# Group means by ScalarE, denominators written before they are read back, and the last blocks added ahead, in four fused layers

## The chip, the cores and the metric

One core of a Trainium2 chip. The kernel is one program that runs four layers one after the other. The time is the device time of an execution in microseconds (us), the median of three runs. The profile is that of one execution.

A core has five engines that run their own instruction streams in order and wait for each other through semaphores: TensorE (PE, matrix products; PEld is its loading of weights), VectorE (DVE), ScalarE (ACT), GpSimd (POOL) and SyncE (SP), which here mostly issues transfers (DMA). Products are written to PSUM, eight banks of 128 x 512 float32; everything else lives in SBUF, 128 partitions wide.

## The reference, cut to what matters

The input is two images of 512 channels and 32 x 32 pixels, float32. Layer 0 is an attention with sampled keys and a small network for its position bias, followed by an MLP; the change leaves its first part alone. Then come

```python
# layer 1: group norm, 8 heads of 64 channels, softmax over 1024 pixels, projection, residual
g = (g - mean) * rsqrt(var + EPS)              # over groups of 16 channels x 1024 pixels
w = softmax(q^T k / sqrt(64)); hh = w v
x = x + proj_w hh + proj_b
# layer 2: group norm, one head of 512 channels
x = x + w_proj softmax(q^T k / sqrt(512)) v + b_proj
# layer 3: no norm, q and k of 64 channels, softmax over the query axis
x = gamma * o + x
```

## The kernel before, in words

Channels lie on partitions, four blocks of 128 (`CC` = 4), and the 1024 pixels (`HW`) along the free axis, in two halves of 512 (`HALF`) or four quarters of 256 (`QUARTER`). All matrix products are float32; each is two records on PE in the profile. Most large products are done by a Strassen-like scheme with seven products instead of eight (`group`, L1463): four PSUM banks x, y, v, z; a product into each, copies and sums of partial results by ACT and DVE (`p1`, `u2`, `p5`, `u3`), then three more products into x, y and v, and an `evict` that adds up the four blocks of the result.

The order of work is written by hand. `in_order` keeps every engine in program order, so an instruction that waits holds all that stand behind it on its engine. What DVE has to do beside the evictions (sums for the seven products, norms, divisions) is put into lists called tracks as (cost, function) pairs with waits between them (a bare number, in us of a virtual clock). `do_chores` is called between products; it advances that clock and issues from each track what is ready, up to a budget of DVE time. So moving or adding one chore shifts what comes after it on its track, and what the other tracks get of the budget.

The places that the change touches:

- `group_norm` (L1212) is a generator. It takes statistics per channel, then forms group means by a product with a constant matrix (`over_group`, L1222): the product goes to a PSUM bank `pg`, the generator yields, and at the next call DVE copies it to `gm` or `var` (L1227). Until then the bank is taken. After the variance, an inverse root is found by four Newton turns of three small DVE operations (L1246), and scale and shift follow. In attention and layer 2 a track made by `statistics` (L1539) advances the generator, with a wait of 6 or 3 us after each late step; in the MLP of layer 0 it is advanced every second chunk.
- `attend` (L1636) is layer 1's attention: 16 iterations, each with eight score products (two 64-row heads side by side), eight exponentials by ACT into tiles of `arena`, and the value products of the iteration before. `divide` (L1687) gets the softmax denominators: products with ones sum over partitions (`den`), ACT copies the rows, four small transfers spread them over partitions (`few`), DVE inverts (`invert`, L1708), the result is written to DRAM (`d`) and read back to 64 partitions each (`r`). Then DVE multiplies `o` by `r`. Of the two halves each is written and read back in turn, all on SP's queue.
- `Weights.total` (L1927) and `divisor` (L1947) do the same for layers 2 and 3. In layer 2 (`shares` False) the exponentials are first added up on DVE to one tile `acc`, and `den` is two products with 512 columns, in two groups of 32 PE columns. It runs four times.
- `weighed` (L1984) is the product of values and weights. Its very last call, second image, second half, second group, uses `evict_last` (L1989): for four 128 x 256 blocks it adds the bias `gb3` and the residual x and where there is one the partial sum, in turn, and stores 128 x 512 blocks to the output with `done` (L2132).

At the end all engines read a flag (is the fast softmax safe?), branch past a general version and meet at a barrier.

Of the kernel before, what the change touches and what calls it, by code (L numbers as in the profile page):

```python
# [12 lines left out]
F32 = mybir.dt.float32  # L13
AF = mybir.ActivationFunctionType
ALU = mybir.AluOpType
# [4 lines left out]
P = 128  # L20
B, C, H, W = 2, 512, 32, 32
HW = H * W
CC = C // P
HALF = 512
# [55 lines left out]
def kernel(ctx: ExitStack, tc: tile.TileContext, a: dict, out: bass.AP):  # L80
    nc = tc.nc
# [14 lines left out]
    def cs(name, i=None):  # L96
        lo, hi = _CONST_AT[name]
        return cst[:, lo:hi] if i is None else cst[:, lo + i : lo + i + 1]
# [1097 lines left out]
    def layers(f, fold_d, t2_b, o2_b, left1, right1):  # L1196
# [3 lines left out]
        small = f.enter_context(tc.tile_pool(name="small", bufs=2))  # L1200
# [11 lines left out]
        def group_norm(x, gname, bname, h, small_psum):  # L1212

            st = small.tile([P, CC, 2, 6], F32, name="st")
            mv = small.tile([P, CC, 2], F32, name="mv")
            for cc in range(CC):
                for half in range(2):
                    nc.vector.bn_stats(st[:, cc, half, :], x[:, cc, half * HALF : (half + 1) * HALF])
                nc.vector.bn_aggr(mv[:, cc, :], st[:, cc].rearrange("p h s -> p (h s)"))
                yield  # L1220

            def over_group(v, name):  # L1222
                pg = small_psum("pg")[:, :CC]
                nc.tensor.matmul(pg, cs("gmean"), v, start=True, stop=True)
                yield
                g = small.tile([P, CC], F32, name=name)
                nc.vector.tensor_copy(g, pg)  # L1227
                return g

            mean = small.tile([P, CC], F32, name="mean")  # L1230
            nc.vector.tensor_copy(mean, mv[:, :, 0])
            yield
            gm = yield from over_group(mean, "gm")
            nc.vector.tensor_sub(mean, mean, gm)
            nc.vector.tensor_mul(mean, mean, mean)
            nc.vector.tensor_add(mean, mean, mv[:, :, 1])
            yield
            var = yield from over_group(mean, "var")
            nc.vector.tensor_scalar(var, var, EPS, None, ALU.add)

            rs = small.tile([P, CC], F32, name="rs")
            square = small.tile([P, CC], F32, name="square")
            nc.vector.tensor_scalar(
                rs.bitcast(mybir.dt.int32), var.bitcast(mybir.dt.int32), -0.5, float(0x5F3759DF), ALU.mult, ALU.add
            )
            for _ in range(4):  # L1246
                nc.vector.tensor_mul(square, rs, rs)
                nc.vector.scalar_tensor_tensor(square, square, -0.5, var, ALU.mult, ALU.mult)
                nc.vector.scalar_tensor_tensor(rs, square, 1.5, rs, ALU.add, ALU.mult)
            sc = small.tile([P, CC], F32, name="sc")  # L1250
            sh = small.tile([P, CC], F32, name="sh")
            nc.vector.tensor_mul(sc, rs, col(gname, 0, CC))
            nc.vector.tensor_mul(sh, gm, sc)
            nc.vector.tensor_sub(sh, col(bname, 0, CC), sh)
            yield
            normed = chan.tile([P, CC, HW], F32, name="hc")
            h.append(normed)
            for cc in range(CC):
                nc.scalar.activation(
                    normed[:, cc, :], x[:, cc, :], AF.Identity, scale=sc[:, cc : cc + 1], bias=sh[:, cc : cc + 1]  # L1260
                )
                yield
# [136 lines left out]
        QUARTER = HALF // 2  # L1399
# [60 lines left out]
        def seven_right(b11, b12, b21, b22, t1, t2, t4, t3=None):  # L1460
            return b11, b21, b22, t4, t1, t2, b12 if t3 is None else t3

        def group(name, nk, n, stationary, moving, evict, slack, plain=False):  # L1463

            third = nk * n / 256

            x, y, v, z = [bank(name)[:, :n] for _ in range(4)]

            def add(out, l, r, start=True):
                for k in range(nk):  # L1470
                    nc.tensor.matmul(  # L1471
                        out,
                        stationary(l, k),
                        moving(r, k),
                        start=start and k == 0,
                        stop=k == nk - 1,
                        skip_group_check=not start,
                    )

            if plain:  # L1480
                for out, (l, r) in ((x, (0, 0)), (y, (6, 0)), (v, (0, 6)), (z, (6, 6))):
                    add(out, l, r)
                    add(out, 1 if l == 0 else 3, 1 if r == 0 else 2, False)
                evict((x, None), (v, None), (y, None), (z, None))
                return
            later, put_off[:] = list(put_off), []
            add(x, 0, 0)
            p1 = temp("p1", n)
            nc.scalar.copy(p1, x)
            if nk > 2:  # L1490
                add(z, 3, 3)
            add(y, 5, 5)
            u2 = temp("u2", n)
            nc.vector.tensor_tensor(u2, y, p1, ALU.add)
            add(v, 4, 4)
            p5 = temp("p5", n)
            nc.scalar.copy(p5, v)
            at_once(later)
            do_chores(third, slack)
            if nk == 2:  # L1500
                add(z, 3, 3)
            add(x, 1, 1, False)
            do_chores(third, slack)
            add(y, 6, 6, False)
            u3 = temp("u3", n)
            nc.vector.tensor_tensor(u3, y, p1, ALU.add)
            add(v, 2, 2, False)
            evict((x, None), (v, u2), (z, u3), (p5, u3))
            do_chores(third, slack)
# [28 lines left out]

        def statistics(steps, wait):  # L1539
            t = track()  # L1540
            for i in range(CC + 5):
                t.append((1.5 if i < CC else 0.5, lambda: advance(steps)))
                if i >= CC:
                    t.append(wait)
            return t
# [141 lines left out]
        def divide(o, acc):  # L1687
# [20 lines left out]
            def invert():  # L1708
                nc.vector.reciprocal(few, few)
                note(few)  # L1710
                d, r = sums_d.tile([2, HW], F32, name="d"), unit("r")
                held.append(r)
                for part in range(2):
                    i = slice(part * 64, part * 64 + 64)
                    nc.sync.dma_start(
                        out=d[part].rearrange("(h q n) -> q h n", h=2, q=64),
                        in_=few[i].rearrange("q (h n) -> q h n", h=2),
                    )
                    nc.sync.dma_start(out=r[i], in_=d[part].partition_broadcast(64))

            def scale():
# [173 lines left out]
        class Weights:  # L1895
# [31 lines left out]
            def total(self):  # L1927
                den, row = bank("den"), temp("row", HALF)
                some = [p.rearrange(self.order, k=2, q=2) for p in (self.p if self.shares else self.acc)]
                n = self.n = min(4, 2 * len(some))  # L1930
                self.few = small.tile([P, 4, HALF // P], F32, name="few2")
                for i in range(2 * len(some)):
                    j = i % n
                    nc.tensor.matmul(
                        den[32 * j : 32 * j + 32],
                        ones[:, :32],
                        some[i // 2][:, i % 2],
                        start=i < n,
                        stop=i + n >= 2 * len(some),
                    )  # L1940
                nc.scalar.copy(row[: 32 * n], den[: 32 * n])
                for i in range(n):
                    nc.sync.dma_start(
                        out=self.few[:, i], in_=row[32 * i : 32 * i + 1].rearrange("o (q n) -> o q n", q=P)
                    )
# [38 lines left out]
        def weighed(name, x, qb, seven_sv, w, bias, done=None, last=False):  # L1984

            n = slice(qb * HALF, (qb + 1) * HALF)
            for g in range(2):

                def evict_last(c11, c12, c21, c22):  # L1989
                    for (base, more), i, q in ((c11, 0, 0), (c21, 1, 0), (c22, 1, 1), (c12, 0, 1)):  # L1990
                        m, at = g + 2 * i, qb * HALF + q * QUARTER
                        dst = x[:, m, at : at + QUARTER]
                        if more is not None:
                            nc.vector.tensor_add(dst, dst, more)
                        nc.vector.scalar_tensor_tensor(dst, base, bias[:, m : m + 1], dst, ALU.add, ALU.add)
                        if q:
                            done(m, n)

                def evict(c11, c12, c21, c22):
                    c = unit("c").rearrange("p (m q n) -> p m q n", m=2, q=2)  # L2000
# [14 lines left out]

                group(
                    name, 4, QUARTER, lambda i, s: seven_sv(i, s)[:, g * P : (g + 1) * P], w.seven,
                    evict_last if last and g else evict, 2.6,
                )
                yield  # L2020

# [286 lines left out]
```

## Time and profile before

| | |
|---|---|
| median of three runs | 3342.02 us (3341.78 to 3342.47) |
| profiled execution | 3342.55 us, its span 3340.7 us |
| PE busy | 3316.0 us, 99% |
| DVE, ACT, POOL busy | 79%, 54%, 20% |
| granted PE clock | 0.999 |
| layer 0 with its MLP | to about 2410 us of the span |
| layer 1 | about 2410 to 2825 and its projection to 2889 |
| layers 2 and 3 | interleaved from 2825 to the end |

Lines of the profile name the source line, the engine and the operation, with the tiles it writes and reads. In the chain of waits, one follows from the last instruction back to what released it; start and length are in us. The wait list gives for each engine what it waited for: total us, times, longest. In the table of stretches a row gives the stretch, its length, and for each engine its busy us and number of instructions, then clock and DMA share. A PE "busy" time has modelled ends, so lengths between starts say more than busy sums.

### The profile page before, as it was taken

The page shows a single profiled execution, that of the slowest core. Times are in us where ns is not written, and L with a number is a line of the kernel's source. Part 1 is how long each engine was busy: PE and PEld are TensorE (multiplying, and loading weights), DVE is VectorE, ACT ScalarE, POOL GpSimd, SP SyncE. Part 2 cuts the span into 40 slices and gives each one's busy share as a digit, 9 for nine tenths or more (in the row PEclk, how much of TensorE's full clock was granted, in tenths as well). Part 3 has the DMA queues.
Part 4 walks back from the last instruction along what each step waited for, and adds up shares of the span by engine and source line. Part 5 has one row for each costly group of instructions (what it writes and reads, how often), then busy time and mean ns, then how long its engine had stood idle before and what let it go on. Part 6 is the DMA issues. An engine that isn't in the chain of part 4 may idle for free.

```text
span 3340.7 us, 60894 instructions
## 1 busy us (share of the span) xinstructions
PE 3316.0 (99%) x24789; PEld 1600.6 (48%) x24789; DVE 2642.5 (79%) x3033; ACT 1812.4 (54%) x2763; POOL 675.3 (20%) x806
## 2 busy tenths in 40 slices
PE   9999999999999999999999999999999999999999
PEld 4333333333333333333333339999953443687777
DVE  7999999999998899999999966455446465665556
ACT  4866877877876677877867642112136245122221
POOL 1333333333333233333333210000000000000000
PEclk9999999999999999999999999999999999999999
DMA  5887787787777587787787741000100000000111
GB/s 178 165 167 150 158 167 159 156 168 154 161 161 157 109 168 152 163 163 158 162 165 155 154 119 58 14 11 11 52 0 14 26 33 16 7 7 4 29 33 36
DMA packets 142993, 343.92 MB, mean 103 GB/s; under 512 B 36976, under 2 KB 51952, under 8 KB 141936
## 3 DMA queue, kind: packets, MB, share of 16 engines
q0 software_dynamic: 68400, 231.26, 37.1%
q1 hardware_dynamic: 71056, 102.12, 10.2%
q10 hardware_dynamic: 3248, 6.56, 0.5%
q8 instruction: 197, 3.23, 0.4%
q14 instruction: 92, 0.75, 0.1%
HBM read 71.46 MB, written 10.83 MB: 25 GB/s over the span
## 4 chain that ended last, share of the span: by engine, by line
PE 96%; DVE 1%; issue 1%; ACT 1%; DMA 0%; ACTq 0%; POOL 0%; DVEq 0%; POOLq 0%
PE z L630 52%; PE pma L135 6%; PE pw L1471 6%; PE pmb L135 5%; PE pmv L1471 4%; PE score L1650 3%; PE pv L1662 3%; PE pm L1471 3%; PE score L1471 3%; PE pmt L1471 1%; PE ppr L1471 1%; PE sim L659 1%; PE pf L135 1%; PE pp L719 1%; PE pma L1374 1%
## 5 line engine op out<-in xcount | busy, mean ns | idle before, releaser
L630 PE MATMUL z<-wa,cpb_w 128*32 128x512 f32 x10880 | 1192.2, 593 | 3.4 <-ACT h L639 3.4
L639 ACT ACTIVATE h<-z,b2h 128x1024 f32<-128x1024 f32 x768 | 852.1, 1115 | 329.2 <-PE z L630 300.4
L613 DVE CUSTOM_DVE_ANT_1 wa<-tab,pairs 128x2048 f32<-128x2048 f32 x340 | 779.9, 2295 | 2.9 <-PE z L630 2.5
L630 PEld LDWEIGHTS z<-wa,cpb_w 128*32 128x32 f32 x10880 | 346.2, 110 | 809.7 <-issue 713.6
L630 PE MATMUL z<-h,cpb_w 128*32 128x512 f32 x5504 | 609.4, 593 | 0.7 <-ACT h L639 0.7
L613 DVE CUSTOM_DVE_ANT_1 h<-tab,pairs 128x2048 f32<-128x2048 f32 x172 | 394.7, 2295 | 1.3 <-PE z L630 1.0
L630 PEld LDWEIGHTS z<-h,cpb_w 128*32 128x32 f32 x5504 | 175.6, 110 | 407.9 <-issue 364.3
L644 DVE SCALAR_TENSOR_TENSOR h<-h,turn,h 128x1024 f32<-128x1024 f32 x256 | 329.8, 1288 | 5.5 <-ACT h L639 5.5
L639 ACT ACTIVATE bridge<-z,b2h 128x1024 f32<-128x1024 f32 x162 | 181.1, 1118 | 118.6 <-PE z L630 118.6
L963 POOL DMA_DIRECT2D bridge<-bridge x150 | 127.6, 850 | 530.6 <-DMA bridge<-h 498.1
L644 DVE SCALAR_TENSOR_TENSOR bridge<-bridge,turn,h 128x1024 f32<-128x1024 f32 x162 | 208.3, 1286 | 5.2 <-ACT bridge L639 5.2
L970 POOL DMA_DIRECT2D bridge<-h x161 | 151.7, 942 | 289.3 <-DVE h L644 175.1
L1314 ACT COPY p<-pma 128x128 f32<-128x128 f32 x80 | 21.4, 267 | 334.4 <-PE pma L135 313.3
L1306 DVE TENSOR_TENSOR upper<-pma,p 128x256 f32<-128x256 f32 x80 | 33.8, 422 | 178.5 <-ACT p L1314 178.4
L1651 ACT ACTIVATE p<-score 128x512 f32<-128x512 f32 x256 | 130.3, 628 | 81.0 <-PE score L1650 79.9
L963 POOL DMA_DIRECT2D h2j<-h2j x90 | 76.2, 847 | 313.0 <-DMA h2j<-h 304.2
L639 ACT ACTIVATE h2j<-z,b2h 128x1024 f32<-128x1024 f32 x94 | 105.1, 1118 | 41.8 <-PE z L630 41.2
L1683 DVE TENSOR_TENSOR acc<-acc,p 128x1024 f32<-128x1024 f32 x96 | 111.2, 1219 | 19.8 <-ACT p L1651 19.5
L1650 PE MATMUL score<-q,k 64*128 64x512 f32 x512 | 120.7, 604 | 1.1 <-DVE gm L1227 1.1
L644 DVE SCALAR_TENSOR_TENSOR h2j<-h2j,turn,h 128x1024 f32<-128x1024 f32 x94 | 121.3, 1290 | 0.0
L1662 PE MATMUL pv<-p,vT 128*64 128x512 f32 x512 | 116.5, 598 | 0.0
L973 POOL DMA_DIRECT2D bridge<-bridge x90 | 108.4, 1204 | 3.2 <-DMA bridge<-bridge 2.5
(463 smaller groups left out, 4369.5 us busy)
## 6 DMA issues: line engine op xcount, KB each, us to landing
bridge<-h POOLq DMA_DIRECT2D x161, 512.0 KB, 5.2
h2j<-h POOLq DMA_DIRECT2D x94, 512.0 KB, 5.5
bridge<-bridge POOLq DMA_DIRECT2D x159, 256.0 KB, 3.6
tab<-slog_d SPq DMA_DIRECT2D x128, 256.0 KB, 5.0
h2j<-h2j POOLq DMA_DIRECT2D x90, 256.0 KB, 3.2
bridge<-bridge POOLq DMA_DIRECT2D x150, 128.0 KB, 5.2
bridge<-bridge SPq DMA_DIRECT2D x90, 128.0 KB, 3.9
bridge<-h2j SPq DMA_DIRECT2D x90, 128.0 KB, 3.7
```

Of the source, the lines that this page charges most:

```text
L135: nc.tensor.matmul(pm, w, m, start=(k == 0), stop=(k == len(pairs) - 1))
L613: nc.vector._custom_dve(TENSOR_ADD_SAT, out=h1, in0=tx.unsqueeze(1).to_broadcast([P, H, 2, W]), in1=ty.unsqueeze(3).to_broadcast([P, H, 2, ...
L630: nc.tensor.matmul(z[point * 32 : point * 32 + 32, n], cpb_w2[:, lo : lo + 32], h1s[point][:, half * 16 : half * 16 + 16, :], start=True, ...
L639: nc.scalar.activation(h2, z, AF.Relu, bias=b2h[:, part : part + 1])
L644: nc.vector.scalar_tensor_tensor(h2, h2, turn[:, part // 2 : part // 2 + 1], parts.pop(part + 1), ALU.mult, ALU.add)
L963: nc.gpsimd.dma_start(out=own[0:P:2], in_=own[1:P:2], accum_op=ALU.add)
L970: nc.gpsimd.dma_start(out=joins[i - 1], in_=other, accum_op=ALU.add)
L1471: nc.tensor.matmul(out, stationary(l, k), moving(r, k), start=start and k == 0, stop=k == nk - 1, skip_group_check=not start,)
L1650: nc.tensor.matmul(sc, ks[m][r, s * P : (s + 1) * P], qs[m][r, n], start=True, stop=True)
L1651: nc.scalar.activation(p[:, part], sc, AF.Exp, scale=64 ** -0.5)
L1662: nc.tensor.matmul(pv[half][part * 64 : part * 64 + 64], vt[s % 4][:, lo : lo + 64], lps[s, half][:, part, :], start=(s == 0), stop=(s == 7),)
L1683: nc.vector.tensor_add(acc[half], acc[half], ps[s, half])
```

## The change

Five edits:

1. `over_group` lets ACT copy the group mean right after the product, before it yields; DVE no longer copies.
2. The Newton turns are cut in two by a yield after the second, and `statistics` gets one step more.
3. In `divide`, both halves' denominators are written before either is read back.
4. In layer 2, `total` sums four blocks of 256 columns in four groups of 32 PE columns instead of two of 512; ACT's copy is 128 x 256 instead of 64 x 512, and four transfers go to `few` instead of two. `divisor` still adds two parts.
5. `group` takes a function `early`, called before the last two products are evicted. In the last call it adds bias and residual to the four blocks, takes the partial sum `u2` as one of the bases, and stores the first block. `evict_last` then adds only what is left, and stores 128 x 256 blocks.

```diff
@@ over_group
                 nc.tensor.matmul(pg, cs("gmean"), v, start=True, stop=True)
-                yield
                 g = small.tile([P, CC], F32, name=name)
-                nc.vector.tensor_copy(g, pg)
+                nc.scalar.copy(g, pg)
+                yield
                 return g
@@ group_norm
-            for _ in range(4):
+            for turn in range(4):
                 nc.vector.tensor_mul(square, rs, rs)
...
+                if turn == 1:
+                    yield
@@ group
             do_chores(third, slack)
+            if early is not None:
+                early(x, u2, z, p5)
             add(y, 6, 6, False)
@@ statistics
-            for i in range(CC + 5):
+            for i in range(CC + 6):
@@ invert
-                for part in range(2):
-                    i = slice(part * 64, part * 64 + 64)
+                halves = [slice(part * 64, part * 64 + 64) for part in range(2)]
+                for part, i in enumerate(halves):
                     nc.sync.dma_start(
                         out=d[part].rearrange("(h q n) -> q h n", h=2, q=64),
                         in_=few[i].rearrange("q (h n) -> q h n", h=2),
                     )
+                for part, i in enumerate(halves):
                     nc.sync.dma_start(out=r[i], in_=d[part].partition_broadcast(64))
@@ total
+                if not self.shares:
+                    self.n = 2
+                    quarters = [(k, q) for k in range(2) for q in range(2)]
+                    for i, (k, q) in enumerate(quarters):
+                        nc.tensor.matmul(
+                            den[32 * i : 32 * i + 32, :QUARTER], ones[:, :32], some[0][:, k, q], start=True, stop=True
+                        )
+                    nc.scalar.copy(row[:, :QUARTER], den[:, :QUARTER])
+                    for i, (k, q) in enumerate(quarters):
+                        nc.sync.dma_start(
+                            out=self.few[64 * q : 64 * q + 64, k],
+                            in_=row[32 * i : 32 * i + 1, :QUARTER].rearrange("o (p n) -> o p n", p=64),
+                        )
+                    return
+                n = self.n = 4
@@ weighed
+                def early(c11, u2, c21, c22):
+                    for base, i, q in ((c11, 0, 0), (c21, 1, 0), (c22, 1, 1), (u2, 0, 1)):
+                        m, at = block(i, q)
+                        nc.vector.scalar_tensor_tensor(
+                            x[:, m, at], base, bias[:, m : m + 1], x[:, m, at], ALU.add, ALU.add
+                        )
+                    done(*block(0, 0))
+
                 def evict_last(c11, c12, c21, c22):
-                    for (base, more), i, q in ((c11, 0, 0), (c21, 1, 0), (c22, 1, 1), (c12, 0, 1)):
-                        m, at = g + 2 * i, qb * HALF + q * QUARTER
-                        dst = x[:, m, at : at + QUARTER]
-                        if more is not None:
-                            nc.vector.tensor_add(dst, dst, more)
-                        nc.vector.scalar_tensor_tensor(dst, base, bias[:, m : m + 1], dst, ALU.add, ALU.add)
-                        if q:
-                            done(m, n)
+                    for more, i, q in ((c21[1], 1, 0), (c22[1], 1, 1), (c12[0], 0, 1)):
+                        m, at = block(i, q)
+                        nc.vector.tensor_add(x[:, m, at], x[:, m, at], more)
+                        done(m, at)
```

In the order of instructions, the products on PE stay the same but for the denominators: layer 2's four, and one in each image's attention that moves two iterations forward. On ACT the copies `gm` and `var` are added and the normalised tiles come one chore later; on DVE the second half of the root follows one chore later, in layer 2 behind eight evictions and sums.

## The prediction

> **What bounds the kernel now.** I read the busy times first, then the matmul engine's own waits, then the chain of waits, the stretches and the order of time around each wait, and last the end of the program.
>
> ```profile
> span 3340.7 us, 60894 instructions
> PE 3316.0 (99%) x24789; PEld 1600.6 (48%) x24789; DVE 2642.5 (79%) x3033; ACT 1812.4 (54%) x2763; POOL 675.3 (20%) x806
> ```
>
> TensorE (PE) is busy in all but 24.7 us. Of these 7.4 come after its last product (3333.24) and most of the rest lie in layer 0, which the change leaves alone. It can win from what is left, from products that run alone or longer around a wait, and from those it makes shorter. The list of who waited for whom, cut to PE in layers 1 to 3, is short:
>
> ```profile
> PE pmv L1471 <- DVE u L1494: 1.7, 2, 1.3
> PE score L1650 <- DVE gm L1227: 1.1, 1, 1.1
> PE score L1471 <- DVE u L1494: 0.7, 1, 0.7
> ```
>
> Columns: total us, times, longest. Three spots, all behind VectorE (DVE). These figures understate the loss, because a matmul that stands alone before or after a wait runs without its partner. The table of stretches gives the true one. An iteration of layer 1's attention, first the one with the wait, then an undisturbed one:
>
> ```profile
> 2728.95:2738.40 9.45, 8.34 (x35) 2.80 (x33) 7.96 (x12) 4.72 (x9) 0.00 (x0) 1.00 0.00 0
> 2747.20:2754.42 7.22, 7.22 (x34) 2.56 (x34) 6.42 (x15) 4.03 (x8) 0.00 (x0) 1.00 0.18 42
> ```
>
> The third number is the length: 9.45 against 7.22 us. Layer 2's value products in the chain (start, us, what), disturbed, and for comparison two undisturbed groups:
>
> ```profile
> 2850.43 4.33 PE pmv L1471 x20
> ...
> 2864.79 24.03 PE ppr L1471 x56
> 3025.58 12.09 PE pmv L1471 x56
> ```
>
> They take 14.36 us from 2850.43 to 2864.79 where 12.09 would do.
>
> **What the Trainium skill says.** "DMA: Bandwidth & Descriptors", Anatomy of one DMA, puts most of a DMA's roughly 2 us fixed cost in the write receipt, heaviest to HBM. The trace agrees and shows more: in the first row group below, a small write holds the read behind it for 3.4 us. "TensorEngine Tiling (Array Packing)", Key Properties and Instruction Overhead: column groups load and multiply independently, a change of mode drains the array, a matmul has a floor of about 60 cycles. The trace shows four groups of 512 columns in the time of two (1.00 against 0.98 us). "Runtime: NRT & Kernel Launch", Instruction fetch mechanics: a taken branch outside the fetched window stalls for a fetch. Here DVE's branch at 3335.5 is followed by its next instruction at 3338.5.
>
> **The change part by part.**
>
> *Group means (over_group).* DVE's gm copy at 2732.69 frees the bank that the sixth score matmul needs; it is behind four 1.2 us additions and weight sums. Now ScalarE (ACT) copies right behind the matmul. In the ACT order it stands after four of the eight exponentials and right after the product's place on PE, so the four exponentials queued behind it, and the score banks and value products that wait for those, are held by its own length alone; a late mean (DVE) would hold PE itself first, as before. It costs some 0.2 us (DVE's took 0.16, no ACT row has this size; 0.1 to 0.4) on an engine busy 4.0 of 7.2 us. PE gets back 9.45 - 7.22 = 2.2 us. Lower end 1.1, the recorded wait; the upper end is the same 2.2, since the next banks were already free. The first image's attention shows no such wait, nor does the MLP: nothing there.
>
> *The root in two halves.* In layer 2 the variance burst (var to sh, 2915.79 to 2919.30) holds DVE, and u at 2924.20 comes late: the matmuls of 2922.95 and 2924.67 stand 1.72 apart instead of 0.86, a loss of 0.86. In the new order the second half (nine operations at 0.197 = 1.77 us) still stands ahead of that u. Only the copy (0.19) and one pt sum (0.46) leave the space before it, 0.65. DVE is busy without a gap over this stretch, so u moves up by that 0.65 at most; I take 0.5 (range 0.2 to 0.86). Everything normalised now comes one chore later. In attention those sums end at 2556.9 and 2778.5 for use at 2603 and 2825, so one more 7.2 us iteration is covered; in layer 2 the steps still stand before the flush. The same shift draws one denominator two iterations forward, to about 2771, where its sums (the additions that end at 2764.2) are done.
>
> *Denominators of layer 1 (invert).* The SP queue, one write, its read, the other write, its read:
>
> ```profile
> 2842.83 0.63 SPq L1715 DMA_DIRECT2D d<-few  x1
> 2846.22 0.46 SPq L1719 DMA_DIRECT2D r<-d  x1
> 2846.76 0.63 SPq L1715 DMA_DIRECT2D d<-few  x1
> 2850.01 0.46 SPq L1719 DMA_DIRECT2D r<-d  x1
> 2853.61 1.23 DVE L1722 TENSOR_TENSOR o<-o,r 128x1024 f32<-128x1024 f32 x1 [2.05 <-DMA r<-d]
> ```
>
> Both writes go out by 2844.1, the later one lands near 2846.9 (3.3 after its issue, as the third row's), so the last read leaves about 3.2 us sooner and lands near 2850.4 to 2851. DVE is free at 2851.55, so its 2.05 us idle vanish. All that follows moves up by as much: u at 2854.75 to 2852.7 (its bank is done by 2852.2), and the second u from 2862.32 to about 2860.3, ending at 2860.7 where the matmul wants it at 2860.8. Of the 2.27 us lost, I take 2.1 (range 1.4 to 2.27). No DMA is added, and nothing else stands in SP's queue there. The seven other divisions get earlier too, with no PE wait to win.
>
> *Denominators of layer 2 (total).*
>
> ```profile
> 2929.25 0.98 PE den L1934 x4
> ```
>
> Two column groups of 512 become four of 256. Two passes of 0.43 plus about 0.12 of switching become two of 0.215 (a 256-column record of pmv takes 12.09/56 = 0.216) plus 0.12: 0.55. Four of these: 4 x 0.43 = 1.7. Bound from issue: eight pairs of load and multiply at the 0.11 us of the 128-column product (5.36/48) would be 0.9, a gain of 0.1 each; but four groups' loads start within 0.16 us in the trace, so I take 0.4 each, 1.6 in all (range 0.4 to 1.7). ACT's copy shrinks from 0.57 to 0.37. SP issues four transfers for two, 2.4 us for 1.15, so `few` is there about 0.65 later (1.25 - 0.4 - 0.2). It is wanted some 0.6 before each write of d, at 2937.0, 2970.7, 3083.1 and 3125.2, after issues that end at 2932.05, 2966.86, 3076.7 and 3110.7. In attention DVE had `few` 1.3 after the last of four such issues (2791.3 to 2792.6). The tightest is the second: 2966.86 + 1.3 + 0.65 = 2968.8 against 2970.7, 1.9 to spare. So it is free; without that cover DVE, which runs in order, would hold the next u and with it PE.
>
> *Last blocks added ahead.* At the end:
>
> ```profile
> 3331.55 0.42 DVE L1506 TENSOR_TENSOR u<-pw,p 128x256 f32<-128x256 f32 x1 [4.69 <-PE pw L1471]
> ...
> 3334.58 0.48 DVE L1995 SCALAR_TENSOR_TENSOR x<-pw,gb,x 128x256 f32<-128x256 f32 x1
> L2220 DVEq COMPARE_BRANCH  x1: 72/72/72, 3335.5 to 3335.5; - x1
> L2220 DVEq EVENT_SEMAPHORE  x1: 21/21/21, 3338.5 to 3338.5; - x1
> ```
>
> PE ends at 3333.24. The four bias additions move into the 4.69 us that DVE idles: the first product is whole by about 3329.8, four at 0.39 end by 3331.4, so u3 keeps its place. After PE's end only one addition of 0.42 is left: 3333.86 instead of 3335.06, 1.2 us. Two 256 KB stores become four of 128 KB, at 0.33 issue each; the last one leaves 1.1 earlier and moves half, some 0.35 less at the 0.75 us that 256 KB take at the 350 GB/s the transfer view shows there. The end needs both DVE's branch (earlier by 1.2) and the last landing (earlier by 1.1 to 1.8; more if its long issue of 0.85 goes to 0.33). I take 1.4 (range 0.7 to 2.0).
>
> Sum: 2.2 + 0.5 + 2.1 + 1.6 + 1.4 = 7.8 us. Against the profiled execution (3342.55, 1.85 around its span) that is 3334.7; the median is 0.53 lower, so 3334.2.
>
> **Rivals.** *Half of it sticks* (the change doesn't do all it says): the denominator's matmuls are bound by issue (0.4 in all), the root's half stays in the way (0.2), only the recorded 1.1 comes back in attention, the end wins 0.7, the division 2.0: 4.4 us, 3337.6, no change that can be told. For it: these are the lower ends, and small matmuls do pay a floor. Against it: the iteration lengths. *More at the end*: the last store loses its slow issue and landing (3.3 us against 2.1 of the others), the end gives 2.3, the root 0.86: 9.1 us, 3332.9. For it: the other stores' 2.1. Against it: DVE's branch allows hardly more than 1.2. *Slower*: the doubled `few` transfers on SP. DVE is in order, so if they come after the addition that wants them, u behind it is late and PE stops, four times. Slack is about 1.9 us at the tightest; the gain of the rest is 6.2, so it decides once PE loses 1.6 us at each, that is with `few` 3.5 us and more behind its present landing. At 4.9 us behind, PE loses 3.0 at each, 12 in all: 6 slower, 3348. Against it: attention already issues four such transfers in the same 2.4 us, and they land 1.3 us after.
>
> **How the numbers follow.** The sum as worked 0.60, half of it 0.22, more at the end 0.12, slower 0.06. 0.2% (6.7 us, so 3335.3) is about what a measurement of this kernel can tell from no change. The sum lies 1.1 us beyond it; of the first case's 0.60 I count 0.55 as faster and 0.05 as within, of the second 0.02 and 0.20, the third all as faster, of the fourth 0.02 within and 0.04 slower. Together: faster 0.69, within 0.2% 0.27, slower 0.04. The range goes from a little below the third case to a little above the second, 3331.8 to 3338.0, and leaves out the slower one and the ends.
>
> **What would show it.** Right: no PE wait on gm; the iteration that holds it at 7.2 to 7.5; the two pmv groups near 12.1; den in layer 2 near 0.55; DVE's last addition about 0.6 us after PE's last matmul. Wrong: den still near 0.9; ACT's exponentials waiting behind a group mean; DVE waiting for `few`; an end that still takes 7.4 us after the last matmul.

## The result, and the profile after

The changed kernel takes 3333.39 us (median of 14 runs, 3331.97 to 3337.02) against 3341.16 us (14 runs, 3339.19 to 3344.57) of the kernel before, side by side: a ratio of 0.9977 with a 95% interval of 0.9970 to 0.9984, 7.8 us faster. The forecast was 3334.2 us, in a range of 3331.8 to 3338.0. The profiled execution took 3333.7 us, with a span of 3331.8 against 3340.7: 8.9 us between the two profiles.

The head of the profile after:

```profile
span 3331.8 us, 60950 instructions
PE 3312.6 (99%) x24805; PEld 1600.7 (48%) x24805; DVE 2641.1 (79%) x3025; ACT 1807.2 (54%) x2771; POOL 674.5 (20%) x806
```

PE's list of waits in layers 1 to 3 is empty: none of the three waits of before is left, and none has come. The place of each gain is read from the chain of waits, which runs on PE nearly throughout, as the distance between two starts that both kernels have:

| stretch, us | before | after | gain | step of the forecast |
|---|---|---|---|---|
| start of the span to the second image's attention | 2703.42 | 2703.13 | 0.29 | none |
| that attention, to the projection's first `pmt` | 121.59 | 119.36 | 2.23 | group means, 2.2 |
| the first two groups of layer 2's value products (`pmv`) | 14.36 | 12.22 | 2.14 | invert, 2.1 |
| layer 2's first score to its first `den` | 40.43 | 39.66 | 0.77 | root in halves, 0.5 |
| that `den` to layer 3's first `den` | 215.06 | 213.40 | 1.66 | total, 1.6 |
| layer 3's first `den` to the flag's product `pn` | 176.52 | 176.52 | 0.00 | none |
| `pn` to the end of the span | 19.87 | 18.06 | 1.81 | last blocks ahead, 1.4 |
| sum | | | 8.90 | 7.8 |

(`pmt` and `ppr` between them take 25.42 and 24.03 in both.) First the table of stretches of the kernel after, over the iteration that holds the group mean (stretch, its length, then the busy times of PE, PEld, DVE, ACT, POOL with their numbers of instructions):

```profile
2728.73:2735.95 7.22, 7.22 (x35) 2.56 (x34) 7.15 (x11) 4.61 (x9) 0.00 (x0) 1.00 0.00 0
```

It was 9.45 long and is 7.22, as an undisturbed one. VectorE is nearly full in it, 7.15 of 7.22, yet nothing on PE waits for it. The chain of waits from the value products on (start, length, what):

```profile
2847.91 12.22 PE pmv L1473 x56
2860.13 24.03 PE ppr L1473 x56
...
2907.12 16.70 PE score L1473 x76
2923.82 0.57 PE den L1940 x8
```

The value products are in one piece, `den` takes 0.57. The order of time of the kernel after, SP's queue and then VectorE, at the last division of layer 1:

```profile
2840.32 1.35 SPq L1719 DMA_DIRECT2D d<-few  x2
2842.22 1.93 SPq L1724 DMA_DIRECT2D r<-d  x2
```

```profile
2848.95 1.22 DVE L1727 TENSOR_TENSOR o<-o,r 128x1024 f32<-128x1024 f32 x1
```

Both writes, then both reads; the multiplication by `r` has no idle time before it, where it had 2.05. Its first read leaves 1.90 us after its first write, and not 3.39 as before: a difference that the change to the order of transfers doesn't make by itself, and that most of the experiments below turn on. The end of the kernel after, first VectorE in the order of time, then by the line of the closing branch (engine, operation, count, duration in ns, first and last start):

```profile
3326.18 0.42 DVE L2023 TENSOR_TENSOR x<-x,pw 128x256 f32<-128x256 f32 x1 [0.51 <-PE pw L1473]
```

```profile
L2247 SPq EVENT_SEMAPHORE  x8: 17/17/17, 3327.5 to 3330.1; - x8
...
L2247 DVEq COMPARE_BRANCH  x1: 72/72/72, 3326.8 to 3326.8; - x1
...
L2247 DVEq EVENT_SEMAPHORE  x1: 21/21/21, 3329.7 to 3329.7; - x1
```

One addition is left behind the last product. VectorE reaches its semaphore at 3329.7, SP, which waits for the stores, its last one at 3330.1.

### The profile page after: what moved, and what is told of

It is laid out like the page before. It is cut to its first block, busy times and chain, and to the rows that moved or that the text cites. A ratio compares the mean times of both kernels' runs of the same rounds, so it can differ in the third digit from the quotient of the medians.

```text
span 3331.8 us, 60950 instructions
## 1 busy us (share of the span) xinstructions
PE 3312.6 (99%) x24805; PEld 1600.7 (48%) x24805; DVE 2641.1 (79%) x3025; ACT 1807.2 (54%) x2771; POOL 674.5 (20%) x806
## 3 DMA queue, kind: packets, MB, share of 16 engines
q8 instruction: 197, 3.23, 0.4%
## 4 chain that ended last, share of the span: by engine, by line
PE 97%; ACT 1%; issue 1%; DVE 1%; DMA 0%; ACTq 0%; POOL 0%; DVEq 0%; POOLq 0%
PE z L630 52%; PE pw L1473 6%; PE pma L135 6%; PE pmb L135 5%; PE pmv L1473 4%; PE score L1654 4%; PE pv L1666 3%; PE pm L1473 3%; PE score L1473 3%; PE pmt L1473 1%; PE ppr L1473 1%; PE sim L659 1%; PE pf L135 1%; PE pp L719 1%; PE pma L1376 1%
```

## The experiments

All but one are the changed kernel with one thing altered (in one of the last two, two things), and each edit is undone alone in one of them; the stretches of the table above are the measure. Totals of single executions say less: the second image's attention starts anywhere between 2702.7 and 2705.3, after a layer 0 that the experiments change little or not at all.

### Group means: who copies, and when

Copied by VectorE after the yield, as before:

```diff
-                g = small.tile([P, CC], F32, name=name)
-                nc.scalar.copy(g, pg)
                 yield
+                g = small.tile([P, CC], F32, name=name)
+                nc.vector.tensor_copy(g, pg)
```

> The changed kernel with its first edit undone: VectorE copies the group mean, one chore after the product. My theory (the bank is held until the late copy): the attention of the second image, from the end of the projection to the first of its value products' followers, goes from 119.4 us back to about 121.6, with a wait of score on gm of some 1.1 us; the score products of layer 2 up to the first denominator lose 0.1 to 0.3 of the 0.77 they won, from the copy alone; everything else as in the changed kernel. Span about 2.3 to 2.6 longer, near 3334.2. Rival (the shifted chores of the split root did it, not the copy): attention stays at 119.4.

3336.64 us. The attention takes 121.58, 2.22 more, and layer 2's stretch to its first `den` 39.85, 0.19 more. PE's wait is back in the wait list (total us, times, longest):

```profile
PE score L1654 <- DVE gm L1227: 1.1, 1, 1.1
```

The recorded wait is 1.1 and the loss 2.2. The other half hides in busy time, as matmuls that stand alone at either side of the wait: in the iteration that the prediction shows, PE is busy for 8.34 us where an undisturbed one has 7.22. The stretch was the right measure.

Copied by VectorE, but ahead of the yield:

```diff
                 g = small.tile([P, CC], F32, name=name)
-                nc.scalar.copy(g, pg)
+                nc.vector.tensor_copy(g, pg)
                 yield
```

> The changed kernel, with VectorE instead of ScalarE copying the group mean, but at once, right behind the product and before the yield. My theory (when it is copied counts, not who copies): the copy then stands behind four additions that end about 4.8 us before the bank is wanted again, so attention stays at 119.4 us, no wait of score on gm; in layer 2 the 0.19 of the copy comes back at most; span within 0.3 of the changed kernel's. Rival (VectorE is too loaded there, the copy must go to ScalarE): attention back at 120.5 to 121.6.

3334.43 us; attention 119.36, value products 12.21, score to `den` 39.65: nothing comes back. What counts is that the copy stands in the queue before the chores, not which engine makes it. For the four small copies here ScalarE is no better than VectorE.

### The root in halves

```diff
-                if turn == 1:
-                    yield
...
-            for i in range(CC + 6):
+            for i in range(CC + 5):
```

> The changed kernel with its second edit undone: the four turns in one piece and one step less. My theory: of the 0.77 us that the score products of layer 2 won up to the first denominator, the copy's leaving gave 0.2 and the split 0.46 to 0.57, so this stretch goes from 39.66 to 40.1 to 40.25, with a wait of score on u of about 0.5; attention stays at 119.4. Rival (the copy alone did it, since the second half still stands ahead of u): the stretch stays at 39.7. Third (the split hides the whole root): 40.4.

3333.77 us. Score to `den` takes 40.22, 0.56 more, and the wait on `u` returns, at 0.5 instead of 0.7:

```profile
PE score L1471 <- DVE u L1494: 0.5, 1, 0.5
```

So the cut is worth 0.56, and the early copy another 0.19 (the first experiment); together 0.75 of the 0.77.

### Layer 2's denominators

Two groups of 512 columns and two transfers, as before:

```diff
-                if not self.shares:
-                    self.n = 2
...
-                    return
-                n = self.n = 4
+                n = self.n = min(4, 2 * len(some))
...
-                nc.scalar.copy(row, den)
+                nc.scalar.copy(row[: 32 * n], den[: 32 * n])
```

> The changed kernel with its fourth edit undone: layer 2's denominators as two products of 512 columns in two column groups. My theory: each of the four goes from 0.57 to 0.98 us, 1.64 in all, and nothing else moves; span near 3333.4. Rival (the shorter copy or the earlier landing of few also counts): more than 1.8.

3336.39 us. In the chain of waits of this kernel:

```profile
2925.31 0.98 PE den L1939 x4
```

Each of the four is 0.41 longer than the 0.57 of the changed kernel, 1.64 in all, and the stretch to layer 3's first `den` is 215.06 again, the figure of before. (The rest of the difference in time lies in layer 0.)

How much room the doubled transfers of `few` have: twice and four times as many pieces, with the same bytes to the same places.

```diff
                     for i, (k, q) in enumerate(quarters):
-                        nc.sync.dma_start(
-                            out=self.few[64 * q : 64 * q + 64, k],
-                            in_=row[32 * i : 32 * i + 1, :QUARTER].rearrange("o (p n) -> o p n", p=64),
-                        )
+                        for s in range(2):
+                            p, c = 64 // 2, QUARTER // 2
+                            nc.sync.dma_start(
+                                out=self.few[64 * q + p * s : 64 * q + p * s + p, k],
+                                in_=row[32 * i : 32 * i + 1, c * s : c * s + c].rearrange("o (p n) -> o p n", p=p),
+                            )
```

With eight:

> The changed kernel, but layer 2's denominators go to few in eight transfers of 32 partitions instead of four of 64. SP needs about 4.8 us to issue them instead of 2.4. My theory: some 1.9 us of slack at the tightest of the four, so VectorE waits for few by about 0.5 there and not at the other three, and TensorE loses 0 to 0.5 us in all. Rival (the slower case of the prediction lies nearer than worked out, or few has much more cover): TensorE loses 1 us or more, or VectorE doesn't wait at all.

3333.85 us, all stretches as in the changed kernel. But VectorE does wait, and for longer than the 0.5 expected. In its order of time, with eight transfers:

```profile
2964.39 0.42 DVE L1496 TENSOR_TENSOR u<-pw,p 128x256 f32<-128x256 f32 x1 [2.83 <-PE pw L1473]
2967.49 0.16 DVE L1971 TENSOR_TENSOR few<-few 128x4 f32<-128x4 f32 x1 [2.68 <-DMA few<-row]
...
2969.50 0.42 DVE L1510 TENSOR_TENSOR u<-pw,p 128x256 f32<-128x256 f32 x1 [1.37 <-PE pw L1473]
```

and the changed kernel at the same place:

```profile
2964.65 0.15 DVE L1969 TENSOR_TENSOR few<-few 128x4 f32<-128x4 f32 x1
...
2969.42 0.42 DVE L1510 TENSOR_TENSOR u<-pw,p 128x256 f32<-128x256 f32 x1 [4.15 <-PE pw L1473]
```

SP's issues end 2.55 later (4.94 us for 2.39), and VectorE waits 2.68: with four transfers `few` comes hardly any earlier than it is wanted. What keeps PE from losing is the idle time behind: 4.15 us in which VectorE waits for the product of its next `u`, cut to 1.37 here.

With sixteen:

> As the one in eight, but sixteen transfers of 16 partitions, about 9.6 us of issuing, so that few lands some 7.2 us later than in the changed kernel. My theory: VectorE waits some 5.3 us at the second denominator and some 4 at the first (its slack is about 2.9), little or nothing at the third and fourth (4 and 12 us of cover); TensorE loses a part of these waits, since its products run ahead of VectorE by up to a group: 3 to 8 us in all, span 3335 to 3340. Rival (VectorE's wait costs TensorE nothing, since the sums behind it have slack): span within 1 us of the changed kernel's.

3343.42 us, against 3342.04 of one execution of the kernel before. From the wait list of layers 2 and 3:

```profile
DVE few L1971 <- DMA few<-row: 15.2, 3, 6.6
PE pmv L1473 <- DVE u L1496: 3.7, 2, 2.7
```

Layer 2's first score to layer 3's first `den` takes 260.6 us for 253.1: 7.5 lost, within the 3 to 8 expected, with issues of 10 us in place of 2.4. So the slower rival exists as a mechanism, and is far from what four transfers do.

### The end

Additions behind the last products again, stored as two blocks of 128x512:

```diff
-                    evict_last if last and g else evict, 2.6, early=early if last and g else None,
+                    evict_last if last and g else evict, 2.6,
```

(with `evict_last` as it was before)

> The changed kernel with its fifth edit undone: the last blocks are added after their products, with two stores of 128 x 512. My theory: from the product of the flag to the end 19.9 us instead of 18.06, the span 1.8 longer, near 3333.6, with the last VectorE operation 1.8 us after the last product instead of 0.5, and the branch and the last store both later. Rival (the end is set by stores only): VectorE later, end no more than 0.5 later.

3335.38 us. From `pn` to the end 19.00 us: 0.94 more than the changed kernel, where 1.8 was expected. The additions ahead, but two wide stores:

```diff
-                    done(*block(0, 0))
...
-                        done(m, at)
+                        if q:
+                            done(m, n)
```

> The changed kernel with the last additions ahead, but the end stored as two blocks of 128x512 as before, not four of 128x256. From the flag's product to the end the changed kernel has 18.06, and 17.7 to 18.2 in the experiments with its end. If VectorE's branch sets the end: 17.9 to 18.3. If the landing of the last store sets it: 18.4 to 19.0, since 256 KB leave last, some 0.35 longer at least.

3334.24 us; 18.13 us. The number lies where I had put VectorE's branch, but that is not what sets the end here. The closing lines of three kernels show it. First this one, then the one with the additions behind, then the kernel before in a second execution (told below):

```profile
L2247 SPq EVENT_SEMAPHORE  x8: 17/17/17, 3328.1 to 3330.8; - x8
...
L2247 DVEq EVENT_SEMAPHORE  x1: 21/21/21, 3331.1 to 3331.1; - x1
```

```profile
L2239 SPq EVENT_SEMAPHORE  x8: 17/17/17, 3329.7 to 3331.2; - x8
...
L2239 DVEq EVENT_SEMAPHORE  x1: 21/21/21, 3332.4 to 3332.4; - x1
```

```profile
L2220 SPq EVENT_SEMAPHORE  x8: 17/17/17, 3336.5 to 3339.5; - x8
...
L2220 DVEq EVENT_SEMAPHORE  x1: 21/21/21, 3338.9 to 3338.9; - x1
```

The spans end at 3332.5, 3333.5 and 3341.2. In the kernel before, in both executions, and in the changed one SP comes last, and the end follows SP's last semaphore by 1.7 us. With the additions behind, VectorE comes last, 1.2 us after SP, and the end follows VectorE by 1.1. With the wide stores VectorE is last too, but by 0.3 only, and the end again follows SP by 1.7. That distance is 1.7 in 13 of the 14 profiled executions; in the one with the additions behind it is 2.3. So the stores set the end in both kernels, and VectorE's branch only in that one experiment.

Counted from `pn` (3314.50 with the additions behind, 3321.03 in the kernel before, 3313.74 in the changed kernel), VectorE's semaphore is at 17.9, 17.9 and 16.0, SP's last at 16.7, 18.5 and 16.4. VectorE moved up by what the edit takes from it. SP waits for the last store. Its size and time from issue to landing, in the first execution of the kernel before, in the changed kernel and with the additions behind:

```profile
out<-x SPq DMA_DIRECT2D x1, 256.0 KB, 3.3
out<-x SPq DMA_DIRECT2D x1, 128.0 KB, 3.4
out<-x SPq DMA_DIRECT2D x1, 256.0 KB, 2.1
```

The last store is late in both kernels; in the changed one the two stores ahead of it land in 1.8. (With the wide stores it takes 3.2 to land, so the doubled size is not what counts.) In the kernel before, its issue is long as well, 0.85 us (0.96 in the second execution) for 0.34 with the additions behind. In those 13 executions a fetch of instructions (the next section tells of them) runs during that store: in the two of the kernel before it begins some 0.7 us ahead of the issue, and the issue ends 0.37 us after the fetch; in the others it begins 0.2 to 0.8 us after the issue. With the additions behind, the fetch is over just before the store is issued. So the fetch is the likely cause of the delay, and the 0.94 sets a delayed end against one that is not delayed. Without the delay VectorE would set the changed kernel's end, at about 16.0 + 1.1 = 17.1, and the edit would be worth some 1.9, by an estimate from these figures.

### Layer 1's denominators: written ahead, or in turn

Each half written and read back in turn, as before:

```diff
-                for part, i in enumerate(halves):
                     nc.sync.dma_start(out=r[i], in_=d[part].partition_broadcast(64))
```

> The changed kernel with its third edit undone: each half written and read back in turn. My theory: the two groups of value products after layer 1 go from 12.22 us back to about 14.3, VectorE waits some 2 us for the read back, nothing else changes; span about 2.1 longer, near 3333.9. Rival (the chores that moved, and not the transfers, brought it): stays near 12.2.

3333.9 us. The value products take 12.55 us (from `pmt`'s start to the score's, 62.00, less the 49.45 of `pmt` and `ppr`), 0.33 more and not 2.1. My reason for the largest uncertain step had fallen. SP's queue and VectorE in the order of time:

```profile
2840.73 0.63 SPq L1719 DMA_DIRECT2D d<-few  x1
2842.63 0.46 SPq L1723 DMA_DIRECT2D r<-d  x1
2843.17 1.40 SPq L1719 DMA_DIRECT2D d<-few  x1
2846.24 0.46 SPq L1723 DMA_DIRECT2D r<-d  x1
```

```profile
2849.69 1.23 DVE L1726 TENSOR_TENSOR o<-o,r 128x1024 f32<-128x1024 f32 x1 [0.24 <-DMA r<-d]
```

The first write holds its read for 1.90 us, not for 3.39 as in the kernel before; the second, which goes out beside a running read-back, for 3.07 as there. VectorE idles 0.24 instead of 2.05. Same order of transfers, 1.5 us apart. Was the slow one an accident of that execution? The kernel before, once more:

> The kernel before once more, in a second profiled execution. In the first, the last division of layer 1 let its first read leave 3.39 us after its write was issued, where e4_read_in_turn, with the same order of transfers, had 1.90; and the last store of the kernel took 3.3 us to land after an issue of 0.85. Theory (that one execution had two slow transfers, which the prediction took for the rule): the read leaves after about 1.9, layer 2's first two value product groups take 12.3 to 12.8 us instead of 14.36, and the stretch from the flag's product to the end is 19.0 to 19.4 instead of 19.87; the other stretches stay (attention 121.6, score to the first denominator 40.4, denominators 0.98). Rival (the slow write belongs to the kernel before): the read leaves after 3.3 to 3.4 again and the groups take 14.2 to 14.5.

3343.0 us. The read leaves 3.58 after its write, the value products take 14.50, `pn` to the end 20.17. The rival was right: the slow write belongs to the kernel before. So something else in its trace must differ at this place. The view of transfers shows it. Over 6 us from 2 us before the write, the kernel before in this second execution (GB/s in 40 slices of 0.15 us; then packets, MB and share of 16 DMA engines by queue):

```profile
GB/s 0 0 0 0 0 0 0 0 0 0 0 0 0 0 0 0 0 0 0 0 0 3 22 110 0 0 0 0 0 2 0 0 0 0 0 0 0 0 0 0
...
q1 hardware_dynamic: 144, 0.00, 1.3%
q8 instruction: 1, 0.02, 1.0%
```

and the changed kernel, over the same 6 us:

```profile
GB/s 0 0 55 0 0 0 0 0 0 0 0 0 0 0 0 0 0 0 0 0 0 3 23 1 0 0 9 19 0 0 109 0 0 0 164 273 273 328 300 219
...
q8 instruction: 1, 0.02, 1.0%
```

The 3, 22 (and 3, 23) are the write's packets, about 1.2 us after its issue. The 110 and 109 are one packet of 16 KB on queue q8, kind "instruction": an engine fetches its next instructions. It holds one DMA engine for about 1 us (1.0% of 16 engines x 6 us = 0.96). In the kernel before it goes out with the write, and a crumb of the write (the 2) trails 0.9 us behind, ahead of a landing 1.6 us late (3.5 us after the issue for 1.9). In the changed kernel the fetch comes 1.2 us after the write's packets, and the read leaves at 1.90.

The same holds over all traces of this case: eight divisions in each of 14, 112 first writes. 102 of them let their read go after 1.86 to 1.94 us. The other ten took 2.25 to 3.85, and each has a fetch between 0.6 and 1.8 us behind its issue: eight times one of q8, and in the two mildest (2.25 and 2.54) one of q14, half as large, at 1.1. Of the q8 fetches from 0.6 to 1.6, all seven met a slow write. Of the four at 1.6 to 1.8 one did (with the two spare writes told of below); later ones never did. Two of the ten show what writing ahead does with a slow write: in the kernels with the late copy and with VectorE's copy it took 3.41 and 3.27 at this very division, and the value products stayed at 12.21.

Two other kinds of transfer in the same traces agree. In the ten kernels that write ahead, where no q8 fetch delayed the first write, the second let its read go after 1.84 to 2.1 us, except for seven with 3.1 to 3.7. These seven have a q8 fetch 0.9 to 1.4 us behind the second write's issue, and no other has one there. And at the end of the ten kernels with the changed end, the third of the four stores landed in 3.7 to 4.0 us in the five where the fetch began 1.1 to 1.2 us behind its issue, and in 1.8 in the five where it began 1.35 to 1.6 behind. No run moves a fetch alone, so this is a coincidence found again and again, not an experiment on the fetch.

The Trainium skill has both halves of a reason. "Runtime: NRT & Kernel Launch", Instruction fetch mechanics, says that each engine's sequencer refills its instructions in 16 KiB blocks through a DMA queue of its own, at a cost "mostly hidden". The profile agrees on the size (197 packets of q8 with 3.23 MB, 16.4 KB each). "DMA: Bandwidth & Descriptors", Queues, rings and completion order, says that a transfer's semaphore lands only after every earlier write of the same DMA engine, across its queues. That fits one packet that delays a neighbour's completion by its own length and more. It is argued, not shown: no view names the DMA engine that a packet used.

Two more kernels delay the writes on purpose, by two spare writes ahead of them, in turn and ahead:

```diff
+                spare = sums_d.tile([2, HW], F32, name="spare")
+                for part in range(2):
+                    nc.sync.dma_start(
+                        out=spare[part].rearrange("(h q n) -> q h n", h=2, q=64),
+                        in_=few[halves[part]].rearrange("q (h n) -> q h n", h=2),
+                    )
                 for part, i in enumerate(halves):
```

> The changed kernel with each half written and read back in turn, and two spare writes of the same size issued ahead of them in every division of layer 1; nothing reads the spare writes. Each costs an issue of 0.63 on SP, so all that follows is 1.26 late or more, since they also fill the DMA queues. Theory (in turn, the last read lands 0.24 after VectorE is free, so that any delay of a write falls through to TensorE): VectorE waits 1.4 to 3.0 us for r at the last division and the two value groups take 13.5 to 15.2 us instead of about 12.5 without the spare writes. Rival (a late write doesn't decide, and the 14.36 of the kernel before had another cause): 12.6 or less.

> The changed kernel as it is, both halves written ahead of reading back, with the same two spare writes ahead in every division of layer 1. Theory (written ahead, the last read lands about 2 us before VectorE is free): the delay of 1.26 is covered, VectorE waits at most 0.6 for r at the last division, and the two value groups stay at 12.2 to 12.8. Rival (the spare writes hold back both orders alike): 13.5 and more.

3337.42 and 3335.06 us. The multiplication by `r`, in turn and then ahead:

```profile
2852.96 1.23 DVE L1732 TENSOR_TENSOR o<-o,r 128x1024 f32<-128x1024 f32 x1 [3.52 <-DMA r<-d]
```

```profile
2850.86 1.22 DVE L1733 TENSOR_TENSOR o<-o,r 128x1024 f32<-128x1024 f32 x1 [1.26 <-DMA r<-d]
```

Both delays came out larger than I had set them, since in both a q8 fetch met the write (3.45 and 3.85 us to its read): with the 1.4 that the spare issues take, some 3.0 us later than undisturbed in turn, and 3.35 ahead. Both numbers lie outside their ranges for that reason, and 13.57 us for the value products is where I had put the rival. The difference between the two is the answer all the same. In turn, the last read left 3.05 us later and that cost 3.28 (15.83 us for 12.55). Ahead, 3.35 cost 1.35 (13.57 for 12.22): writing ahead covers the first 2 us.

## Why the prediction was right, and where it wasn't

*Group means, 2.2.* Right: 2.23 between the profiles, 2.22 when undone. The iteration lengths gave it, the recorded wait of 1.1 would not have. ScalarE's copies took 0.15 to 0.20 us, as estimated. That it must be ScalarE was no part of the gain.

*Root in halves, 0.5 (0.2 to 0.86).* Right in kind: the stretch won 0.77, of which the split 0.56, for the 0.5 put on it. The other 0.19, from copying early, I had counted only as a part of the 0.65 that can leave the space before `u`.

*Invert, 2.1.* Right in number, wrong in what the number rests on. The step took 3.4 us between a small write and its read as what such a write costs, from this division alone. The seven divisions before it have 1.9 for their first writes, and the roughly 2 us of the Trainium skill, cited beside it (its section gives them for transfers that GpSimd issues; these are SP's), was the better guide. The 3.3 for the second write is right for writing in turn (3.0 to 3.3 in all eight divisions), but written ahead it too took 1.87. With 1.9 the order of transfers alone is worth 0.33, and that is what undoing it in the changed kernel cost. The other 1.8 came from a write that was held up, in both profiled executions of the kernel before, with a fetch of instructions beside it. Writing ahead covers such a delay up to 2 us; in the changed kernel the fetch has also moved off the write. Either would have been enough for this part: 12.21 with a slow write ahead, 12.55 with a fast one in turn. I had named no such condition: that something other than the order of transfers held the write was not among the rivals.

*Total, 1.6 (0.4 to 1.7).* Right: 1.66. Passes of 0.215 and 0.12 of switching gave 0.55, measured 0.57; the bound from issue (0.9) didn't hold for four column groups. The step's cover was mis-sized. It put `few` 1.9 us ahead of its use at the tightest, and it is there just in time; it missed that VectorE then idles 4.15 us anyway, so that PE would begin to lose only when `few` is about 4 us late. Two errors that cancel in the number, not in the reasoning.

*Last blocks ahead, 1.4 (0.7 to 2.0).* The term was too small: 1.81 between the profiles. VectorE's last addition ends 1.37 earlier, counted from `pn` (12.86 for 14.23, from 1.2 estimated), and its semaphore 1.7; but SP's stores come last in both kernels, and these moved by 1.9. The last store leaves 1.37 earlier and its issue shrank from 0.85 to 0.33; half the bytes brought nothing (3.4 us to land for 3.3). The rival *More at the end* put 2.3 there for the slow store, and I had turned it down because the branch would not allow more. The branch did not hold the end. Undoing the edit in the changed kernel cost only 0.94, in the one execution whose last store escaped a fetch and landed in 2.1.

*The sum.* The five steps measured 8.6 between the profiles, for 7.8. That the medians differ by just 7.8 is in part luck: two terms were too small, a third rests on a wrong reason, and the profiled executions differ by 8.9. Undone one at a time in the changed kernel, the edits are worth 2.41, 0.56, 0.33, 1.64 and 0.94: 5.9. The missing 2.7 are the slow write (1.8) and the slow last store (0.9), which the kernel before has and the two experiments that undo these edits don't. Whether they are there in every run of the kernel before is not visible in runs without a profile, and stays open. No view names the engine that fetched. The counts point to TensorE: in both kernels' profiles it starts 254 matmuls and weight loads on average from one q8 fetch to the next, with a standard deviation of 13 to 14%, and for every other engine that number varies by 45% and more.

*Rivals.* Half of it sticks (3337.6) fell: the denominators were not bound by issue, and the attention got back the whole 2.2. More at the end (3332.9) was right that the stores set the end, though it won 1.81 there and not 2.3; the measured 3333.39 lies between it and the forecast. Slower (3348) needs not twice but some eight times the transfers: sixteen of them lost 7.5 us.

## What to carry to other kernels

Read a wait's cost from the length of the stretch it lies in against an undisturbed one, not from the wait list: 1.1 recorded, 2.2 lost. Before a duration goes into a sum, compare its row with the same instruction's other occurrences; one that stands apart has a cause of its own, and a change elsewhere in the program may move that cause. And a late transfer costs nothing until it has used up both its own slack and the idle time behind the instruction that waits for it, so look at that next idle time before putting a price on the wait.

## What was not expected of the hardware

A fetch of instructions is one packet of 16 KB, and in these traces small transfers beside it complete late. A write of 4 KB with no read-back running let its read go after 3.1 to 3.7 us instead of 1.9 wherever a fetch of q8 went out 0.7 to 1.5 us after its issue, and a store of 128 KB landed in 3.7 to 4.0 us instead of 1.8 with one 1.1 to 1.2 us after. SP's issues are held too: of its 29 issues in layers 1 to 3 of the 14 traces that took over 1 us (0.3 to 0.6 are usual), 27 end 0.3 to 0.4 us after the end of a q8 fetch. The place of a fetch depends on the whole program: the kernels that copy four columns on VectorE instead of ScalarE have it on the last division's first write, the changed one has it 2.5 us after the issue. A small write that leaves beside a running read-back of 256 KB takes 2.9 to 4.1 us to release its read, with or without a fetch.
